# One outgoing transfer instead of four, four returning transfers instead of one: the block exchange through DRAM in an attention and expert kernel

## The chip, the cores and the metric

The kernel runs on one core of a Trainium2 chip. The metric is the device time of one execution in microseconds (us), over several executions of the same program. The core has five instruction queues that run beside each other and meet only at semaphores: TensorE (PE, matrix products), VectorE (DVE), ScalarE (ACT), GpSimd (POOL) and SyncE (SP). SP does no arithmetic here; it starts transfers. ACT computes, and it can start transfers too.

## The reference

32 sequences of 112 tokens of width 256 attend to their own context of 375 rows. The context rows and the latents together make 487 keys, with 16 heads of width 64. A mixture of eight experts follows, of which each token uses two. All of it is float32.

```python
x_ = layer_norm(x, ln_m_g, ln_m_b); lat = layer_norm(latents, ln_l_g, ln_l_b)
q  = lat @ Wq;  k, v = split(concat([x_, lat], 1) @ Wkv, 2)
dots = einsum('bhid,bhjd->bhij', q, k) * scale
attn = softmax(dots, axis=-1)
out  = einsum('bhij,bhjd->bhid', attn, v) ... @ Wout
x = x + tanh(g_xattn[0]) * out
# then: gate, top 2 of 8 experts, gelu MLP of width 1024, weighted sum, residual
x = x + tanh(g_ffn[0]) * ffn(layernorm(x))
```

The change touches only how the softmax weights `attn` are turned, so that the keys lie on the partitions for the product with `v`.

## The kernel before

**Stages.** The attention part runs as 64 stages (`period` in the code), each made of two of the 128 half steps `n`. A stage works for two "sets" `s` (one per sequence of a pair), each with two pairs of heads, `p` = 0 and 1. Work is pipelined over the stages. In one stage the kernel

1. multiplies the weights of the stage's own two sets with the values (`attend`, line 600, 64 products), and ACT copies the result out (line 617);
2. computes the scores of the next stage's two sets (`scores`, line 536), takes the negated row maxima on DVE (line 546), and takes the exponentials on ACT (`exps`, line 555, eight instructions per stage);
3. lets PE compute key, value and query projections for later stages (lines 373, 434, 439). Their results are gathered by ACT copies (line 475), DVE additions (line 484) and POOL additions (line 487);
4. normalises the exponentials on ACT (`norm`, line 569, two instructions for each set and `p`; the four are named n00, n01, n10, n11 after set and `p`) and turns them in 32x32 blocks on DVE (`turn_blocks`, line 574: t00, t01, t10, t11);
5. sends the turned blocks to DRAM (`send_blocks`, line 580; s0 and s1 for the two sets) and takes them back, in the next stage, with the blocks on other partitions (`take_blocks`, line 587).

**What the exchange does.** After `turn_blocks` each 32x32 block is transposed in itself, but still lies at its old place. A set is a tile `ex` of 128 partitions and 2048 floats (8 KB on each partition, 1 MB together). Block (a, k), where a is the group of 32 partitions and k a group of columns, has to go to partition group k, column group a. That move is done by a write to a DRAM tile `turned` and a read back into `exT`. Before the change the write did the sorting: four transfers, one for each a, of 2 KB runs, into `turned[k, j, a, n]`. The read back was one plain transfer of 128 runs of 8 KB.

**Order.** The order on every engine is written out by hand. The table `PLAN` has ten entries, five for each half step, and gives the place of each piece between the others. Its first lines are

```python
PLAN = ("k1 q0 q1", "k6 v1 n00", "v6 v5 n01 t00", "k7 v7 n10 t01 k2 s0", "v2 k5 n11 t10", "v3 t11 s1", ...)
```

The two takes of a stage stand right behind the second entry, in the main loop:

```python
if h == 1 and not late and n < LAST - 2:
    for s in (n, n + 1):
        take_blocks(s)
```

So on an engine that takes part in `take_blocks`, its instructions come after those of "k6 v1 n00" and ahead of those of "v6 v5 n01 t00". On ACT the first piece behind that point is the copy of v5 (line 475), which POOL's addition (line 487) waits for; then come n01, n10, the copy of k5, and n11. Before the change all sends and takes are on SP, in the same order as the loads of the inputs (`load`, lines 274 and 278), of the expert weights that are prepared beside the attention (`piece_in`, lines 1375 and 1379), their results going out (`piece_out`, lines 1415 and 1419), and the residual rows (lines 626 and 651).

**Buffers.** There are three `ex` tiles, two `exT` tiles and four `turned` tiles. A take has to wait until `attend` has read the old `exT` and until the send of its own set has landed. `attend` of a stage waits for both takes that belong to it.

Of the kernel before, what the change touches and what calls it, by code (L numbers as in the profile page):

```python
# [23 lines left out]
def kernel(  # L24
# [20 lines left out]
    nc = tc.nc  # L45
# [38 lines left out]
    KTB, EXB, ETB = 4, 3, 2  # L84
# [18 lines left out]
    QB, QW, Q = 4, 32, S // 4  # L103
# [17 lines left out]
    turned = [dram.tile([QB, QW, QB, 2 * NCK * 2 * QW], F32, name=f"turned_{n}") for n in range(4)]  # L121
# [70 lines left out]
    if True:  # L192
# [309 lines left out]
        pss, nmx, sm, exT = {}, {}, {}, {}  # L502
# [3 lines left out]
        exs = [const.tile([P, QB, 2, NCK, 2, QW], F32, name=f"ex_{n}") for n in range(EXB)]  # L506
# [68 lines left out]

        def send_blocks(n, eng=nc.sync):


            for a in range(QB):
                eng.dma_start(  # L580
                    turned[n % 4][:, :, a, :].rearrange("k j n -> j k n"),
                    exs[n % EXB][a * QW : (a + 1) * QW].rearrange("j k q c h r -> j k (q c h r)"),
                )

        def take_blocks(n):
            exT[n] = soft.tile([P, QB, 2, NCK, 2, QW], F32, tag="exT", name=f"exT_{n}", bufs=ETB)
            nc.sync.dma_start(
                exT[n].rearrange("p a q c h r -> p (a q c h r)"),
                turned[n % 4].rearrange("k j a n -> (k j) (a n)"),
            )  # L590

        def attend(j):

# [930 lines left out]
        norm(1, 0)  # L1524
        turn_blocks(0, 1)
        send_blocks(0)
        units[0, 1][6]()
        norm(1, 1)
        turn_blocks(1, 0)
        weight_sums(0, 2)  # L1530
        units[0, 1][1]()
        turn_blocks(1, 1)
        send_blocks(1)
        units[1, 0] = seven(1, 0, 0)
        for kv, k in PROLOGUE:
# [17 lines left out]
        for n in range(LAST):  # L1553
# [17 lines left out]
            def step(what, period=period, beside=beside, qn=qn):  # L1571
                s, p = int(what[1]), int(what[-1])
                if what[0] == "q":
                    for j in qn:
                        q_unit(j // NG, j % NG + NG * s)
                elif what[0] in "kv":
                    at = beside[what[0]]
                    if at[1] < (UNITS, UNITS // 2)[at[0]]:
                        if at not in units:
                            units[at] = seven(*at)  # L1580
                        units[at][p - 1]()
                elif period + 1 < UNITS:
                    s += 2 * (period + 1)
                    if what[0] == "n":
                        norm(s, p)
                    elif what[0] == "t":
                        turn_blocks(s, p)
                    else:
                        send_blocks(s)
# [24 lines left out]
            k = n - 44  # L1614
# [89 lines left out]
            for h in range(5):  # L1704
                for what in PLAN[5 * late + h].split():
                    step(what)
                do(pe[h])
# [3 lines that stand above are left out]
                if h == 1:  # L1711
                    do(after)
                if h == 1 and n == LAST - 2:
                    for s in (n, n + 1):
                        take_blocks(s)
                if h == 4:
                    break
                then_ = soon_[:]
                del soon_[:]
                do(then_)  # L1720
                for part in dve[h]:
                    part()

                if outgoing and (h % 2 == 0 or n > LAST - NG):
                    outgoing.pop(0)()
                if extra and not (late and h > 1 and isinstance(extra[0], tuple)):
                    do(extra.pop(0))
# [3 lines left out]
        r, _ = route_parts(g, nc.vector)  # L1731
# [130 lines left out]
```

## Time and profile before

| | |
|---|---|
| median of three runs | 1907.17 us (1904.93 to 1913.34) |
| the profiled execution | 1907.72 us, span 1905.9 us |
| granted TensorE clock | 0.997 |
| PE busy | 1876.3 us, 98% of the span |
| DVE busy | 1353.5 us, 71% |
| ACT busy | 1136.4 us, 60% |
| POOL busy | 992.5 us, 52% |
| sends (line 580) | 512 transfers of 256 KB, all from SP |
| takes (line 587) | 128 transfers of 1024 KB, all from SP |
| DMA queue q1 (SP's) | 247232 packets, 413.31 MB, 73.6% of 16 engines' span |
| DMA queue q10 (ACT's) | 2288 packets, 2.12 MB, 0.4% |

Times on the page are microseconds. In a list of waits, a line names who waited, for whom, the total, how often, and the longest wait. In a timeline a line has the start, the length, the engine, the source line, the operation, output and input, and the number of instructions merged into it; in brackets stands the idle time of the engine just before and what ended it. "SPq" and "ACTq" rows are the issuing of transfers on the queues of SP and ACT; their length is the time for which that queue was occupied with issuing, and not the time until the data landed. In the tile view, three numbers with slashes are the shortest, median and longest duration in ns. In the view by windows, each line is one stretch with the busy time of PE, PEld, DVE, ACT and POOL, the granted clock, the share for which the DMA engines were busy, and the rate in GB/s.

The attention stages lie between about 60 and 1490 us and are some 20.5 to 27 us long each. The expert part follows.

### The profile page before, as it was taken

What the parts mean: (1) busy time and instruction counts of PE and PEld (TensorE: products, weight loads), DVE (VectorE), ACT (ScalarE), POOL (GpSimd) and SP (SyncE); (2) the same over time, 40 slices, a digit from 0 to 9 for tenths busy, and PEclk for the clock granted to TensorE, in tenths of its full rate; (3) what the DMA queues carried; (4) which work ended last, traced back from release to release, by engine and by line L of the source; (5) the groups of instructions that cost most, each with busy time, mean ns of one, the idle gap of its engine ahead of it and who ended that gap; (6) DMA issues with size and microseconds to landing.
All of it is one profiled execution on the core that took longest, in us unless ns stands there. A gap on an engine that the chain in (4) does not pass through costs nothing. (4 is left out here: it accounts for less than half of the span.)

```text
span 1905.9 us, 38258 instructions
## 1 busy us (share of the span) xinstructions
PE 1876.3 (98%) x12560; PEld 1433.5 (75%) x12560; DVE 1353.5 (71%) x2868; ACT 1136.4 (60%) x2718; POOL 992.5 (52%) x1475
## 2 busy tenths in 40 slices
PE   8999999999999999999999999999999999999998
PEld 4667777677777676777676777677677999999887
DVE  6787878787877878787878787878776477844111
ACT  5767666666776666667766666666756334434333
POOL 6433333435445746585556655753334588877212
PEclk9999999999999999999999999999999999999999
DMA  7777766767788888798979898896668786897872
GB/s 202 193 229 209 214 196 198 205 182 205 226 227 265 253 246 251 230 280 250 271 224 284 233 268 242 252 265 195 198 184 256 244 240 180 245 336 232 231 205 46
DMA packets 261049, 433.23 MB, mean 227 GB/s; under 512 B 30728, under 2 KB 149072, under 8 KB 244464
## 3 DMA queue, kind: packets, MB, share of 16 engines
q1 hardware_dynamic: 247232, 413.31, 73.6%
q0 software_dynamic: 11328, 15.33, 4.2%
q10 hardware_dynamic: 2288, 2.12, 0.4%
q8 instruction: 101, 1.65, 0.3%
q14 instruction: 100, 0.82, 0.1%
HBM read 301.37 MB, written 172.28 MB: 249 GB/s over the span
## 5 line engine op out<-in xcount | busy, mean ns | idle before, releaser
L555 ACT ACTIVATE ex<-bank,nmx 128x512 f32<-128x512 f32 x512 | 343.6, 697 | 85.7 <-DVE nmx L546 85.2
L569 ACT ACTIVATE ex<-ex,rc 128x512 f32<-128x512 f32 x512 | 342.7, 721 | 76.1 <-DVE rc L566 75.4
L546 DVE TENSOR_REDUCE nmx<-bank 128x1 f32<-128x487 f32 x512 | 298.6, 655 | 85.9 <-PE bank L536 83.6
L574 DVE STREAM_TRANSPOSE ex<-ex 128x1024 f32<-128x1024 f32 x256 | 314.9, 1230 | 19.5 <-ACT ex L569 15.7
L487 POOL TENSOR_TENSOR vv<-tmpv,vv 128x512 f32<-128x512 f32 x64 | 82.1, 1282 | 404.1 <-ACT vv L475 403.4
L536 PE MATMUL bank<-kT,qTs 64*128 64x487 f32 x1024 | 236.3, 588 | 3.0 <-DVE kvT L365 1.7
L600 PEld LDWEIGHTS bank<-exT,vv 128*64 128x64 f32 (+1 forms) x4096 | 198.9, 137 | 30.9 <-issue 22.6
L600 PE MATMUL bank<-exT,vv 128*64 128x112 f32 (+1 forms) x4096 | 213.0, 261 | 2.3 <-DMA exT<-turned 1.6
L617 ACT COPY outT<-bank 128x256 f32<-128x256 f32 (+3 forms) x160 | 40.0, 314 | 263.9 <-PE bank L600 258.8
L434 PE MATMUL bank<-tT,wkv_s 128*128 128x487 f32 x378 | 186.3, 575 | 0.5 <-ACT ex L555 0.5
L439 PE MATMUL bank<-wkv_s,tT 128*128 128x256 f32 x768 | 186.7, 379 | 0.0
L439 PEld LDWEIGHTS bank<-wkv_s,tT 128*128 128x128 f32 x768 | 144.8, 190 | 43.3 <-issue 21.4
L1164 POOL DMA_INDIRECT out_dram<-y,xs x60 | 93.5, 1558 | 154.0 <-DVE y L1191 77.9
L536 PEld LDWEIGHTS bank<-kT,qTs 64*128 64x128 f32 x1024 | 98.8, 187 | 99.2 <-issue 69.9
L1405 POOL TENSOR_TENSOR piece<-piece 128x128 f32<-128x128 f32 x256 | 116.9, 457 | 89.7 <-DMA piece<-in_L_ffn_w_dram 78.3
L439 PE MATMUL bank<-wkv,kvT 128*128 128x256 f32 x512 | 132.0, 380 | 0.8 <-ACT ex L555 0.6
L439 PEld LDWEIGHTS bank<-wkv,kvT 128*128 128x128 f32 x512 | 94.6, 190 | 50.5 <-issue 33.9
L484 DVE TENSOR_TENSOR kT<-bank,kT 128x487 f32<-128x487 f32 x189 | 120.8, 640 | 14.0 <-POOL kT L487 7.5
L434 PE MATMUL bank<-kvT,wkv 128*128 128x487 f32 x252 | 130.1, 598 | 0.0
L484 DVE TENSOR_TENSOR vv<-bank,vv 128x512 f32<-128x512 f32 x192 | 128.2, 668 | 1.8 <-POOL vv L487 0.2
L1219 ACT ACTIVATE h<-h,b 128x256 f32<-128x256 f32 x160 | 66.1, 495 | 91.9 <-DVE h L1230 53.2
L373 PEld LDWEIGHTS bank<-kvT,wq_sb 128*128 128x128 f32 x512 | 96.2, 188 | 28.9 <-issue 17.0
(296 smaller groups left out, 3718.2 us busy)
## 6 DMA issues: line engine op xcount, KB each, us to landing
turned<-ex SPq DMA_DIRECT2D x512, 256.0 KB
exT<-turned SPq DMA_DIRECT2D x128, 1024.0 KB
w<-in_L_ffn_w_dram SPq DMA_DIRECT2D x132, 256.0 KB
w_s<-ws SPq DMA_DIRECT2D x80, 256.0 KB
w_t<-ws SPq DMA_DIRECT2D x80, 256.0 KB
w_b2x<-in_L_ffn_w_dram SPq DMA_DIRECT2D x38, 512.0 KB
ws<-piece SPq DMA_DIRECT2D x64, 256.0 KB
cin<-in_ctx_dram SPq DMA_DIRECT2D x32, 336.0 KB
```

Of the source, the lines that this page charges most:

```text
L373: nc.tensor.matmul(ps, lhsT=wq_sb[:, k, i * P : (i + 1) * P], rhs=kvT[g][:, k, :, SC:NK], start=(k == 0), stop=(k == KD - 1),)
L434: nc.tensor.matmul(ps, lhsT=w[:, 0, i * P : (i + 1) * P], rhs=x[:, :NK], start=True, stop=True)
L439: nc.tensor.matmul(ps[:, c, :], lhsT=x[:, (2 * h + c) * P : (2 * h + c + 1) * P], rhs=w[:, 1, i * P : (i + 2) * P], start=True, stop=True,)
L484: nc.vector.tensor_tensor(v[o], ps, v[r], ALU.add)
L536: nc.tensor.matmul(ps[:, :NK], lhsT=qT[b // 2, i][r, b % 2].rearrange("p a i -> p (a i)"), rhs=kT[b, i][r, :], start=True, stop=True,)
L546: nc.vector.tensor_reduce(nmx[b, i][:, j : j + 1], pss[b, i][j][:, :NK], AX.X, ALU.max, negate=True)
L555: nc.scalar.activation(exs[n % EXB][:, :, p, :, j, :], ps[j].rearrange("p (c k r) -> p k c r", c=NCK, r=QW), AF.Exp, bias=nmx[b, i][:, j : ...
L569: nc.scalar.mul(t, t, rc[:, j : j + 1])
L574: nc.vector.transpose(t, t)
L600: nc.tensor.matmul(ps[y * DH : (y + 1) * DH, r, x * S : (x + 1) * S].rearrange("p (a i) -> p a i", a=QB), lhsT=vv[j // 2, c // 2][:m, c % ...
L1164: add = nc.gpsimd.indirect_dma_start(out=outf, out_offset=bass.IndirectOffsetOnAxis(ap=xs[t][:, b, D + 1 : D + 2].bitcast(I32), axis=0), i ...
L1405: nc.gpsimd.tensor_tensor(o, l, r, op) for o, l, r, op in ops
```

## The change

The sorting moves from the write to the read. The tile `turned` is now read as `[a, j, k, n]`: a send writes the whole `ex` tile as it lies, in one transfer of 128 runs of 8 KB. A take is four transfers, one for each destination group of 32 partitions, and each of the four gathers 128 runs of 2 KB. The first two are issued by SP and the last two by ACT. The same bytes move in each direction, and nothing else of the kernel is edited.

```diff
         def send_blocks(n, eng=nc.sync):

-
-            for a in range(QB):
-                eng.dma_start(
-                    turned[n % 4][:, :, a, :].rearrange("k j n -> j k n"),
-                    exs[n % EXB][a * QW : (a + 1) * QW].rearrange("j k q c h r -> j k (q c h r)"),
-                )
+            eng.dma_start(
+                turned[n % 4].rearrange("a j k n -> (a j) (k n)"),
+                exs[n % EXB].rearrange("p k q c h r -> p (k q c h r)"),
+            )

         def take_blocks(n):
             exT[n] = soft.tile([P, QB, 2, NCK, 2, QW], F32, tag="exT", name=f"exT_{n}", bufs=ETB)
-            nc.sync.dma_start(
-                exT[n].rearrange("p a q c h r -> p (a q c h r)"),
-                turned[n % 4].rearrange("k j a n -> (k j) (a n)"),
-            )
+            for k in range(QB):
+                eng = (nc.sync, nc.scalar)[k // 2]
+                eng.dma_start(
+                    exT[n][k * QW : (k + 1) * QW].rearrange("p a q c h r -> p a (q c h r)"),
+                    turned[n % 4][:, :, k, :].rearrange("a j n -> j a n"),
+                )
```

Per stage SP issues six of these transfers instead of ten, and ACT four instead of none.

## The prediction

> **What bounds the kernel now.** I read the page first (who is busy, who moves the bytes), then the list of waits, then one stage as a timeline, then DMA by windows.
>
> ```profile
> PE 1876.3 (98%) x12560; PEld 1433.5 (75%) x12560; DVE 1353.5 (71%) x2868; ACT 1136.4 (60%) x2718; POOL 992.5 (52%) x1475
> ```
>
> TensorE has work in 98% of the span, so a shorter transfer can win only what PE waits for transfers. Anything that makes another engine late is paid in full once its cover is used up.
>
> ```profile
> POOL vv L487 <- ACT vv L475: 403.4, 60, 13.5
> ACT ex L569 <- DVE rc L566: 75.4, 87, 2.4
> DVE nmx L546 <- PE bank L536: 83.6, 45, 3.2
> PEld bank L434 <- ACT ex L555: 45.5, 64, 1.3
> ```
>
> The first line: once in nearly every stage POOL stands still until ACT has copied v5, the copy that stands right behind the new ACT transfers. The third is the cover: in 45 of some 62 stages DVE is idle for 1.86 us (83.6/45) before its first row maximum; in the other 17 it comes there late already. The fourth: in all 64 stages the first weight load behind the scores waits for an exponential, which waits for a maximum. A late DVE is therefore felt by PE in the same stage.
>
> ```profile
> L580 SPq DMA_DIRECT2D turned<-ex x512: 302/691/1981, 34.0 to 1468.8; - x171
> L587 SPq DMA_DIRECT2D exT<-turned x128: 319/412/1715, 41.3 to 1479.8; - x128
> ...
>   DMA exT<-turned: 3.4, 2
> ```
>
> The tile view of the exchange: a send of 128 runs of 2 KB occupies SP for 0.69 us, a take for 0.41. The last line is how long the products waited for takes: twice, 3.4 us together. The exchange is hidden.
>
> ```profile
> 273.57 1.33 ACT L569 ACTIVATE ex<-ex,rc 128x512 f32<-128x512 f32 x2
> 274.81 0.58 ACT L475 COPY vv<-bank 128x512 f32<-128x512 f32 x1
> 275.30 1.33 ACT L569 ACTIVATE ex<-ex,rc 128x512 f32<-128x512 f32 x2
> 277.32 1.22 DVE L574 STREAM_TRANSPOSE ex<-ex 128x1024 f32<-128x1024 f32 x1
> 284.34 0.13 DVE L523 MEMSET bank<- 128x25 f32 x3
> 286.59 3.52 DVE L546 TENSOR_REDUCE nmx<-bank 128x1 f32<-128x487 f32 x6 [2.12 <-PE bank L536]
> 282.24 3.30 PE L600 MATMUL bank<-exT,vv 128*64 128x112 f32 x64
> ```
>
> One stage (261.6 to 282.2, from products to products). n00 runs at 273.57, the v5 copy at 274.81, n01 at 275.30. The new transfers stand between the first two lines. DVE has no gap from 274.94 to 284.4, then waits 2.12 us for scores.
>
> ```profile
> 274.00:275.00 1.00, 1.00 (x5) 0.73 (x4) 0.83 (x3) 1.00 (x3) 0.00 (x0) 1.00 0.97 410
> ...
> 280.00:281.00 1.00, 1.00 (x5) 0.67 (x4) 1.00 (x2) 1.00 (x2) 0.92 (x2) 1.00 0.99 197
> ```
>
> Last two columns: DMA share and GB/s. Takes (274) run at 410, sends (280) at 197, each with the DMA engines full. From 276 to 279 they are nearly idle.
>
> **The change part by part.** The sum is made against the profiled execution, 1907.7 us, which is 0.5 above the median of 1907.2.
>
> *Removed from SP:* 512 sends become 128, and 128 takes become 256. Per stage SP loses 8 x 0.69 + 2 x 0.41 = 6.3 us of issuing and gets back 2 sends at 0.4 (the row of the 8 KB takes) and 4 takes at 0.69 = 3.6. The 2.7 us are worth nothing on the path: SP stood waiting for turned blocks for 545.5 us (89 waits at line 580 for DVE), and nothing waits for SP but transfers, whose lateness cost PE 3.4 us at line 600 and 1.8 us of weight loads. Gain: 0 to 5 us; I take 0, since neither wait recurs by stage.
>
> *The sends' runs grow from 2 to 8 KB.* No row writes 8 KB runs to DRAM. Bounds: 197 GB/s as now, or 410 as the 8 KB reads have it: 1.05 MB in 5.3 or 2.6 us. The take of the next stage is the earliest reader, some 5 us behind the last send, so both are hidden: 0.
>
> *Added to ACT:* four issues per stage, 256 in all. They stand behind n00 and, in one stage of four, behind the two activations of line 361, and ahead of the v5 copy, n01, n10, the k5 copy and n11. Price of four issues together:
>
> ```profile
> 2.29 0.36 ACTq L1435 DMA_DIRECT2D wkv<-in_L_xattn_Wkv_dram  x1
> 2.69 0.44 ACTq L1435 DMA_DIRECT2D wkv_s<-in_L_xattn_Wkv_dram  x1
> 3.17 1.72 ACTq L1435 DMA_DIRECT2D wkv<-in_L_xattn_Wkv_dram  x2
> ...
> 1515.13 2.24 SPq L1092 DMA_DIRECT2D w_t<-ws  x4
> ...
> 741.18 4.54 SPq L580 DMA_DIRECT2D turned<-ex  x4
> ```
>
> Four on ACT's own queue take 0.36 + 0.44 + 1.72 = 2.52 us; four reads of 2 KB runs on SP 2.24; four sends behind a busy queue 4.54, the upper end. The lower end is four single ones at 0.343 (the shortest issue on ACT, at line 936): 1.4. I take 2.5, the row of this queue. Part runs beside ACT's arithmetic: at 1672.11 a transfer is issued 0.3 us before the activations of 1671.51 end, so the queue runs ahead by 0.3 to at most one activation (0.67); I take 0.5. So v5 and all behind it on ACT is 2.0 us later, with 0.7 and 4.5 as ends. The takes' own waits add nothing here: the send landed long before, and `attend`, which frees exT, ended some 9 us earlier.
>
> *Who waits for ACT.* First DVE: the transpose t01 (277.32) needs n01 (ends 276.63), cover 0.7. In other stages that cover is 0.1 (t01 at 256.17, n01 ends about 256.1) or 1.2 (207.37 against 206.13). With 0.7 as the mean, DVE's tail is 1.3 us later. In the 45 stages with 1.86 us of idle time that is absorbed; in the 17 without it reaches the maxima, the exponentials and PE: 17 x 1.3 = 22 us. Ends: 0 at a delay of 0.7; at 4.5 us, 3.8 x 17 + (3.8 - 1.86) x 45 = 152 us.
>
> Second POOL: from 713.42 (v5's addition) to 723.50 it has no gap, and DVE waits 0.21 us for it at 721.02. In such stages (pieces, tokens and input sums on POOL, about every third, 20) the whole 2.0 arrive, against covers of 1.4 to 2.0, and 0 in three of them: 0.4 on average, 8 us. Ends: 0, and 20 x (4.5 - 1.4) = 62, which overlaps the 152.
>
> *PE's own waits.* The first product of each set waits for four transfers instead of one, six more wait instructions per stage. One is 51 ns at line 600 where the trace has it: 62 x 6 x 0.051 = 19 us if none runs ahead, 0 if all do (the weight loads' short waits, 0.44 us each at line 600, cost the products next to nothing). I take 6. The exponentials lose as many waits (17 to 38 ns each) on ACT, which is worth nothing on PE's path.
>
> *Transfers that come later.* The ACT takes start some 10 us later in the stage than SP's do. By the stage above they are issued from 274.4 to 277 and needed at 282.24 (first set) and 283.1 (second). At 410 GB/s 1.05 MB take 2.6 us, at 197 GB/s, the rate of 2 KB runs in the sends, 5.3. With 2.6 us from the last issue to the landing (sends end issuing at 265.69, the take that needs them is issued at 268.33) they land by about 279.6, or 281 to 282.3. Hidden by the first, just hidden by the second. I take the first, since reads of 2 KB runs (w_s and w_t, 1518 to 1520) move 382 GB/s. Cost 0; the other end is a rival below.
>
> Sum: 22 + 8 + 6 = 36 us: 1907.7 + 36 = 1943.7, or 1943 against the median.
>
> *A rule against the change.* The Trainium skill (DMA: Bandwidth & Descriptors, Rules for kernel authors) advises against splitting a transfer into disjoint partition groups: the parts run on the same engines and one transfer for all partitions is better. The rows above have the engines full with one take (0.97), which agrees, but they hold no split take. By the rule the split brings 0 in transfer time and only adds issues, so the sum stays; by the trace alone it could also have cost 2.7 us per set, the difference of the two rates. A second statement there (Anatomy of one DMA) is a time of 2.0 us and 1 us for each 436 KB, for the other kind of queue: by an estimate from it the last 256 KB would land 2.6 us after issue, and the late rival would not happen at all.
>
> **The rivals.**
>
> *Hidden after all (not slower).* If ACT's queue takes the issues while n00 still runs and each costs the single price, the delay is 0.7 us and ends in t01's cover of 0.7. For it: 0.343 single issues, and idle DMA from 276 to 279. Against it: no row of four stays under 1.5 us. It decides at a delay of 0.7. Time: 1907 to 1913; 1910.
>
> *Late takes.* If gathered 2 KB reads run at 197 GB/s and share the engines with weight pieces or s0, the products wait 1 to 3 us in each stage, in place of, not beside, most of the tail's delay: 62 x 1 to 62 x 3, 1970 to 2094. Against it: the 382 GB/s row, and that s0 is itself later by ACT's delay.
>
> *Faster.* Shorter sends end the 5.2 us of waits for exT: 1902, if ACT's cost is hidden too. To be told from no change it must win 9.5 us, so another 4 us would have to come from POOL's 78.3 us of waiting for weight pieces, which PE has felt little so far: 1898.
>
> **How the numbers follow.** About 0.5%, 9.5 us, can be told from no change. Chances: forecast mechanism (1918 to 1985) 0.52; hidden 0.22; late takes or an ACT delay near its upper end 0.19; faster 0.07. The hidden case is all within 0.5%. The range must reach into the hidden case and part of the late one: 1906 to 2010 leaves out the faster case and a little over half of the last one. Faster 0.07, same 0.22, slower 0.71.
>
> **What would show it.** ACTq rows of line 587 with about 2.5 us per four; the gap between n00 and v5 grown by about 2 us; POOL's wait for ACT at L487 up by 60 x 2 = 120 us; the line "DVE nmx <- PE" clearly below 83.6; PE's wait for exT still a few us; 8 KB sends visible as a changed rate where 197 stands now. Wrong it would be if the ACT gap is under 1 us, or if products wait for exT in every stage.

## The result, and the profile after

The changed kernel takes 1932.26 us (median; 1929.57 to 1934.45), the kernel before on the same chip 1907.76 us (1904.93 to 1913.34). The ratio is 1.0124, with a 95% interval of 1.0096 to 1.0153: slower by some 24.5 us. The profiled execution took 1934.26 us, its span is 1932.6 us, 26.7 more than the span before.

Page of the changed kernel, engines and the two DMA queues (packets, MB, share of 16 engines' span):

```profile
PE 1886.4 (98%) x12560; PEld 1437.9 (74%) x12560; DVE 1357.2 (70%) x2868; ACT 1139.2 (59%) x2718; POOL 991.5 (51%) x1475
...
q1 hardware_dynamic: 210368, 346.18, 60.6%
q10 hardware_dynamic: 39152, 69.24, 16.9%
```

The same bytes of these two queues now keep the DMA engines busy for 77.5% of the span instead of 74.0%. One of the two directions has become dearer.

List of waits of the changed kernel:

```profile
POOL vv L487 <- ACT vv L475: 442.1, 57, 15.3
DVE nmx L546 <- PE bank L536: 85.6, 44, 5.0
PE bank L600 <- DMA exT<-turned: 11.6, 15, 2.0
```

POOL waits 39 us more for ACT's v5 copy (403.4 before), not 120. DVE's wait for scores has not shrunk (83.6 before): DVE comes to its maxima as early as it did. The products at line 600 now wait for takes.

Tile `exT` of the changed kernel (shortest, median, longest in ns, first and last start; then idle time of its engines before the instructions on that tile, and how often):

```profile
L587 ACTq DMA_DIRECT2D exT<-turned x256: 309/442/1734, 50.4 to 1502.0; - x128
...
  DMA exT<-turned: 17.3, 21
```

3.4 us in two waits has become 17.3 us in 21, products and weight loads together; PE's own part is 1.6 us before and 11.6 now. The median issue on ACT takes 0.44 us.

Timeline of ACT in the stage that the prediction showed (now 265.2 to 285.8):

```profile
277.12 0.31 ACTq L587 DMA_DIRECT2D exT<-turned  x1
277.13 0.72 ACT L569 ACTIVATE ex<-ex,rc 128x512 f32<-128x512 f32 x1
277.47 0.45 ACTq L587 DMA_DIRECT2D exT<-turned  x1
...
278.04 0.85 ACTq L587 DMA_DIRECT2D exT<-turned  x2
278.93 0.59 ACT L475 COPY vv<-bank 128x512 f32<-128x512 f32 x1 [0.47 <-issue]
```

The four issues occupy the queue from 277.12 to 278.89. They begin together with n00, not behind it, and run beside it for 1.3 us. From the start of n00 to the v5 copy it is 1.80 us, against 1.24 before (273.57 to 274.81): the copy is 0.56 us later. Over the 33 stages in which this copy follows n00 directly, the median of the same time is 1.99 us, 0.75 more than before, and the longest 3.60.

Windows of the same stretch:

```profile
268.00:269.00 1.00, 1.00 (x15) 0.64 (x12) 0.00 (x0) 0.47 (x3) 1.00 (x2) 1.00 0.96 385
...
274.00:275.00 1.00, 1.00 (x8) 0.96 (x7) 0.26 (x2) 1.00 (x5) 0.00 (x0) 1.00 1.06 201
...
281.00:282.00 1.00, 1.00 (x6) 0.70 (x5) 1.00 (x1) 0.95 (x2) 0.97 (x1) 1.00 1.06 217
```

Sends (268) now move at 385 GB/s, takes from SP (274) at 201 and from ACT (281) at 217, with the DMA engines full in all three. Before, the takes ran at 410 and the sends at 197. The slow rate has changed sides: it lay on the sends, which nobody waits for soon, and lies on the takes, which the products wait for.

**Where the 26.7 us lie.** I took the first product of each of the 64 stages from the timelines and compared the stages one by one (before the change they are 19.8 to 30.7 us long). Stages without weight pieces have the length that they had, to 0.01 us in most (20.17, 21.07, 28.03, 21.26, 20.62 us in both kernels); of stages 1 to 25, five are longer, by 1.9 us together. The loss by part of the span, for this kernel and for those of the experiments below whose parts were compared:

| us more than the kernel before | stages 0-25 | 26-51 (pieces) | 52-61 | 62 | behind the start of 63 | span |
|---|---|---|---|---|---|---|
| the change | 4.6 | 15.1 | -1.2 | 4.3 | 3.9 | 26.7 |
| all takes on SP (e1) | 2.0 | 3.7 | -0.7 | 3.2 | 6.2 | 14.5 |
| ACT in piece stages only (e9) | 0.2 | 17.8 | -0.6 | 2.7 | 5.2 | 25.4 |
| ACT outside of them only (e10) | 1.7 | 7.6 | -1.4 | 5.3 | 7.7 | 20.9 |
| all on SP, last pair as before (e11) | -0.2 | 6.4 | -0.6 | 1.5 | 6.1 | 13.2 |
| pieces and last pair as before (e12) | 3.1 | 0.3 | 1.3 | 1.4 | 0.2 | 6.3 |

The table sets single executions beside one of the kernel before that was among its faster ones: 1907.72 us, where the median of that kernel beside e9 to e12 is 1911.43. By the medians e12, for one, is 1.6 us slower and not 6.3.

One stage with pieces shows how. Weight loads of TensorE in the kernel before, from the first product of stage 46, through its first score, to the first product of stage 47:

```profile
1102.76 3.09 PEld L600 LDWEIGHTS bank<-exT,vv 128*64 128x64 f32 x64 [0.72 <-issue]
1106.50 0.19 PEld L536 LDWEIGHTS bank<-kT,qTs 64*128 64x128 f32 x2 [0.21 <-issue]
...
1123.83 0.29 PEld L600 LDWEIGHTS bank<-exT,vv 128*64 128x64 f32 x6 [0.72 <-issue]
```

The same in the changed kernel:

```profile
1116.60 0.80 PEld L600 LDWEIGHTS bank<-exT,vv 128*64 128x64 f32 x16 [1.34 <-issue]
1119.56 3.77 PEld L600 LDWEIGHTS bank<-exT,vv 128*64 128x64 f32 x48 [2.16 <-issue]
1123.99 0.19 PEld L536 LDWEIGHTS bank<-kT,qTs 64*128 64x128 f32 x2 [0.21 <-issue]
...
1141.31 0.77 PEld L600 LDWEIGHTS bank<-exT,vv 128*64 128x64 f32 x16 [0.72 <-issue]
```

From the scores to the next products it is 17.33 us before and 17.32 after, although ACT issues four transfers in between. All that is lost is lost among the products: 64 loads in one run become 16, a gap of 2.16 us, and 48 slower ones. The second set's blocks had not landed. They are on their way from 1104.69 on: SP issues its half, then two pieces, and ACT its half at 1107.22 to 1110.55. Issues of SP in this stage, then windows:

```profile
1104.69 1.96 SPq L587 DMA_DIRECT2D exT<-turned  x4
1106.81 2.54 SPq L1375 DMA_DIRECT2D piece<-in_L_ffn_w_dram  x2
...
1108.00:1110.00 2.00, 2.00 (x9) 1.43 (x8) 1.85 (x4) 0.63 (x2) 0.00 (x0) 1.00 1.06 186
...
1114.00:1116.00 2.00, 2.00 (x7) 0.95 (x5) 2.00 (x5) 1.08 (x3) 1.92 (x3) 1.00 1.07 197
```

Engines full without a gap, at 186 to 206 GB/s in all four windows of these 8 us. Both halves are 2.1 MB, or 10.5 us at 200; the pieces add 0.26 MB and 1.3 us; from 1104.7 that ends at 1116.5, and the products were due at 1116. In fact the second set's products started at 1119.59: from 1115.35 on the next send and a piece going out move beside the rest. In the kernel before, a window of this stage has 402 GB/s, at which the same 2.1 MB take 5.2 us:

```profile
1094.00:1098.00 4.00, 4.00 (x16) 2.84 (x16) 3.31 (x7) 3.14 (x6) 2.85 (x5) 1.00 1.00 402
```

The 48 products are also slow because TensorE's granted clock fell to half just there:

```profile
1119.59 3.96 PE L600 MATMUL bank<-exT,vv 128*64 128x112 f32 x48 [1.98 <-DMA exT<-turned]
...
1119.20:1122.60 3.40, 3.01 (x33) 3.04 (x35) 0.41 (x4) 0.00 (x0) 3.10 (x6) 0.50 1.04 407
```

At full clock 48 such products take 2.53 us (stage 63, at 1512.46), so some 1.4 of the 3.65 us that the products of this stage lost are the clock's.

Over stages 26 to 51, what the products of line 600 lost inside their run sums to 10.3 us, what they lost in front of the first one (a gap above 0.72 us, as the 1.34 above) to 3.2. Together that is 13.5 of the 15.1 us, in the products of eight stages (26, 27, 30, 34, 38, 42, 46 and 50). The rest, 1.6 us in stages 43 and 51, is all that ACT's delay can have cost there.

In these eight stages SP issued its first take 11.6 to 14.7 us ahead of the products, and 14.8 us or more ahead in every other stage from 2 to 62 but number 54. There it was 12.1 us, but the only piece is one going out ahead of the takes, and none comes in behind them; the stage is 0.05 us longer. So both the short lead and the pieces seem to be needed.

**The clock elsewhere.** Stretches at half clock, of 3.4 us or a multiple, stand at a few places in every trace, the one before too. In the first stage ten score products wait for DVE; the change, and then e12, which has the same code there:

```profile
66.54 3.97 PE L536 MATMUL bank<-kT,qTs 64*128 64x487 f32 x10 [1.88 <-DVE kvT L365]
...
67.70 2.71 PE L536 MATMUL bank<-kT,qTs 64*128 64x487 f32 x10 [1.92 <-DVE kvT L365]
...
67.90:74.70 6.80, 6.80 (x15) 3.73 (x12) 3.32 (x6) 5.60 (x18) 0.00 (x0) 0.50 0.55 117
...
67.90:74.70 6.80, 6.80 (x29) 4.17 (x28) 4.81 (x9) 6.31 (x20) 0.00 (x0) 1.00 0.66 149
```

The first stage is 27.3 to 27.6 us long in the change and in e1, e6 and e7, with 6.8 us at half clock in it; 25.7 before and in e5, with 3.4; and 24.0 to 24.3 in e8 to e12, with none. So nearly all of the 1.9 us that the change loses in this stage is the clock's. Why one execution falls to half clock behind an idle time of 1.9 us and another does not is open.

Stage 62 lost its 4.3 us to half clock (1494.6 to 1501.5, up to 3.4 us) and to a wait for gathered expert rows, which was 1.25 us before:

```profile
1496.58 1.12 PE L1115 MATMUL bank<-ident,xs 128*128 128x128 f32 x4 [4.42 <-DMA xs<-xg]
```

For the takes of the last pair the products of the change waited 1.34 us, 1.59 before. Why the rows came later was not settled.

### The profile page after: what moved, and what is told of

It reads as the page before. It is cut to its first block, busy times and chain, and to the rows that moved or that the text cites. A ratio compares the mean times of both kernels' runs of the same rounds, so it can differ in the third digit from the quotient of the medians.

```text
span 1932.6 us, 38353 instructions
## 1 busy us (share of the span) xinstructions
PE 1886.4 (98%) x12560; PEld 1437.9 (74%) x12560; DVE 1357.2 (70%) x2868; ACT 1139.2 (59%) x2718; POOL 991.5 (51%) x1475
## 5 line engine op out<-in xcount | busy, mean ns | idle before, releaser
L546 DVE TENSOR_REDUCE nmx<-bank 128x1 f32<-128x487 f32 x512 | 298.4, 655 | 85.9 <-PE bank L536 85.6
L600 PE MATMUL bank<-exT,vv 128*64 128x112 f32 (+1 forms) x4096 | 214.9, 262 | 12.1 <-DMA exT<-turned 11.6
L1405 POOL TENSOR_TENSOR piece<-piece 128x128 f32<-128x128 f32 x256 | 116.9, 457 | 46.4 <-DMA piece<-in_L_ffn_w_dram 34.8
```

The lines of the kernel that those rows point to most:

```text
L546: nc.vector.tensor_reduce(nmx[b, i][:, j : j + 1], pss[b, i][j][:, :NK], AX.X, ALU.max, negate=True)
L600: nc.tensor.matmul(ps[y * DH : (y + 1) * DH, r, x * S : (x + 1) * S].rearrange("p (a i) -> p a i", a=QB), lhsT=vv[j // 2, c // 2][:m, c % ...
L1405: nc.gpsimd.tensor_tensor(o, l, r, op) for o, l, r, op in ops
```

## The experiments

**e1: all takes on SP.** Layout and transfers of the change, without ACT.

```diff
-                eng = (nc.sync, nc.scalar)[k // 2]
+                eng = nc.sync
```

> All four takes of a set are issued by SyncE, otherwise the changed kernel. Theory A (late takes: ScalarE's half is issued some 10 us into the stage, moves at about 200 GB/s because its 2 KB runs are gathered, and lands after the products are due where weight pieces share the engines): the takes start as early as in the kernel before, the waits of the products for exT fall from 17.3 us to under 6 us, and the time returns to 1905 to 1913 us. Theory B (ScalarE's issuing delays its copies, VectorE and GpSimd, and so TensorE): the time returns too, 1905 to 1913. Theory C (2 KB gathered reads cost DMA time whoever issues them): it stays at 1925 or above.

Measured: 1922.78 us (1921.51 to 1923.61), ratio 1.0064 (1.0047 to 1.0080). Half of the loss stays without a single issue on ACT. The windows at 273 to 277 have 201 to 238 GB/s at a DMA share of 1.02 to 1.09: the rate belongs to the layout, whoever issues. By the table, the stages with pieces lose 3.7 us, all inside the products, and the last pair 3.2. There PE's first 16 products come behind a gap of 4.44 us (0.72 before), and its timeline goes on with the other 48, at half clock (1493.6 to 1503.9):

```profile
1500.46 4.16 PE L600 MATMUL bank<-exT,vv 128*64 128x112 f32 x48 [3.07 <-DMA exT<-turned]
```

Here the products of the last pair stand in front of their data (3.07 us, 1.59 before). So the theory that ACT's queue is the whole cost falls.

**e2: the old layout, its take split.** Sends and layout of the kernel before; each take becomes four transfers of 32 partitions with runs of 8 KB, two of them on ACT.

```diff
-            nc.sync.dma_start(
-                exT[n].rearrange("p a q c h r -> p (a q c h r)"),
-                turned[n % 4].rearrange("k j a n -> (k j) (a n)"),
-            )
+            for k in range(QB):
+                eng = (nc.sync, nc.scalar)[k // 2]
+                eng.dma_start(
+                    exT[n][k * QW : (k + 1) * QW].rearrange("p a q c h r -> p a (q c h r)"),
+                    turned[n % 4][k],
+                )
```

> The kernel before with its sends and layout, but each take split into four transfers of 32 partitions, two of them from ScalarE at the place of the changed kernel. Its reads are contiguous runs again. Theory A: the late half moves at about 400 GB/s, lands 2 to 3 us earlier, the waits for exT stay under 6 us, 1906 to 1915 us, while ScalarE's queue still issues four transfers per stage. Theory B: the issuing is the same, so it is as slow as the changed kernel, 1925 to 1940. If 32 partitions and not the runs make the reads slow, the DMA windows show about 200 GB/s in the takes and it is slow by theory A too.

Measured: 2087.13 us (2080.31 to 2093.08), ratio 1.0934 (1.0913 to 1.0954). No theory had that. Two things come out of it. First, a window in which only ACT's queue moves bytes, its takes of 8 KB runs (224 GB/s over 283 to 286), with the engines full:

```profile
285.00:286.00 1.00, 1.00 (x5) 0.68 (x4) 1.00 (x4) 0.66 (x2) 0.80 (x2) 1.00 0.98 197
```

8 KB runs in groups of 32 partitions move at 197, and the same runs in one transfer of 128 partitions at 410 in the kernel before. So it is not the length of the runs. Second, the waits of the two queues:

```profile
SPq L589 <- DMA exT<-turned: 308.9, 41, 13.9
...
SPq L580 <- DMA exT<-turned: 107.9, 64, 11.2
```

SP stands 417 us before issues until earlier takes have landed, and ACT's v5 copy up to 7.3 us for the same reason. The granted clock of this execution is 0.969, against 0.997 before, so a part of its loss is the clock's. In the program as built, the transfers share eight semaphores in rotation, so that one can wait for the landing of the one eight before it, whichever queue that went by. With 16 slow transfers per stage on two queues the two hold each other up. That this rotation is the reason of the waits is inferred from the rows; what supports it is e5, which also has 16 per stage, on one queue, and loses nothing.

**e3: ACT's half earlier.** The two transfers per set go ahead of the stage's loop, right behind the exponentials; SP's half stays.

```diff
+            if not late and n < LAST - 2:
+                for s in (n, n + 1):
+                    take_blocks(s, range(2, 4))
             for h in range(5):
...
-                        take_blocks(s)
+                        take_blocks(s, range(2))
```

> The changed kernel with ScalarE's two transfers of each set issued about 3 us earlier in its order, right behind the eight exponentials, ahead of the copies of k1 and v1 and of n00; SyncE's half stays. Theory A: about 3 us of lateness go, the longest waits for exT (2 to 3.6 us per stage) vanish, 1912 to 1922 us. Theory B: four issues still stand ahead of v5's copy and now also ahead of k1's and v1's, so 1930 or more.

Measured: 1996.52 us (1995.25 to 1999.26), ratio 1.0454 (1.0436 to 1.0471). The products wait for takes only twice now (4.1 us), but ACT stops. Its timeline, where three of the four transfers are out by 591.49:

```profile
597.91 0.31 ACTq L588 DMA_DIRECT2D exT<-turned  x1
598.26 0.57 ACT L475 COPY kT<-bank 128x487 f32<-128x487 f32 x1 [6.83 <-DMA exT<-turned]
```

The fourth transfer could not be issued before earlier data have landed, and it stands in ACT's instruction stream. All of ACT's arithmetic behind it waits 6.8 us. In the windows 592 to 598 both halves are issued, and 172 to 196 GB/s move with the engines full. By queue it is one after the other: from 592 to 594 SP's moves 0.38 MB and ACT's 0.01, from 595 to 598 SP's 0.02 and ACT's 0.55. A second queue with other partition groups added nothing to the slow rate here.

**e4 and e6: ACT later, without transfers.** All takes on SP as in e1, and in the place of ACT's issues some copies of 128 x 128 that nobody reads: eight of them (2.59 us in ACT's timeline, the v5 copy 2.49 us later), or two (0.63 us, 0.54 later).

```diff
-                eng = (nc.sync, nc.scalar)[k // 2]
+                eng = nc.sync
...
                     for s in (n, n + 1):
                         take_blocks(s)
+                    for _ in range(8):
+                        nc.scalar.copy(busy, ones)
```

> All four takes from SyncE, as in the first of these, and in the place of ScalarE's four issues eight small copies of a constant into a spare tile, about 2 us of ScalarE time per stage: the delay that the prediction assumed, without any late transfer. Theory B as predicted: 36 us over the first of these, about 1943. Theory A: a delay of 2 us is nearly absorbed by VectorE's idle time in most stages; 1908 to 1925.

> All takes from SyncE and two small copies (about 0.5 us) instead of eight in the place of ScalarE's issues: the size of the gap that the changed kernel really shows ahead of v5's copy. Theory: a delay of this size is absorbed, 0 to 6 us over the kernel with all takes on SyncE, 1921 to 1929. If the delay costs in proportion, 73 x 0.5/2.1 = 17 us, 1940.

Measured: with eight 1995.65 us (1994.14 to 1999.56), ratio 1.0446 (1.0429 to 1.0464); with two 1928.01 us (1924.16 to 1931.86), ratio 1.0096 (1.0073 to 1.0119). Against e1 that is 73 us and 5 us. So a delay of 2.49 us cost 1.15 us in each of some 63 stages, and one of 0.54 us next to nothing in most stages: plain stages keep their lengths but for numbers 13 and 14 (0.7 and 1.4 us, part of it at half clock, 377.8 to 381.2). The cover behind ACT is real and lies between the two. The change's own delay, 0.56 us in the stage shown and 0.75 in the median, is near the lower of the two.

**e5: split by columns.** The kernel before, each take in four transfers that reach all 128 partitions, with runs of 2 KB, all from SP.

```diff
+            for a in range(QB):
+                nc.sync.dma_start(
+                    exT[n][:, a].rearrange("p q c h r -> p (q c h r)"),
+                    turned[n % 4][:, :, a, :].rearrange("k j n -> (k j) n"),
+                )
```

> The kernel before with its sends, each take split into four transfers of all 128 partitions by columns instead of by partitions: 128 runs of 2 KB, 8 KB apart in DRAM, all from SyncE. It separates two readings of the 200 GB/s that the changed kernel's takes show. If short gathered runs are slow: about 200 GB/s in the DMA windows right behind the takes. If transfers that touch only 32 partitions are slow, which the earlier run with 8 KB runs into 32 partitions at about 200 GB/s speaks for: 380 to 420 GB/s. Its time is not the point; 1908 to 1930.

Measured: 1910.54 us in one run, with 1909.46 for the kernel before on that chip. Its windows while takes move:

```profile
273.00:274.00 1.00, 1.00 (x7) 0.87 (x6) 0.54 (x2) 1.00 (x4) 0.00 (x0) 1.00 1.01 309
...
276.00:277.00 1.00, 1.00 (x5) 0.70 (x5) 1.00 (x3) 0.81 (x2) 0.94 (x1) 1.00 0.98 377
```

Four transfers of 2 KB runs reach 291 to 377 GB/s if each touches all partitions, and some 200 if each touches 32. The shorter runs cost something (410 for one take of 8 KB runs), the partition groups cost the half. Splitting as such, with four waits for each product instead of one, costs nothing that the time shows.

**e7: more bytes beside the takes.** The change, and in the plain stages two transfers of 256 KB from DRAM to DRAM behind SP's takes.

```diff
+                    if 6 <= n <= 40:
+                        for c in range(2):
+                            nc.sync.dma_start(spare[c], w1[n % E, c * P : (c + 1) * P, :512])
```

> The changed kernel with two extra copies of 256 KB from DRAM to DRAM in each of the 18 stages from the fourth to the twenty-first, where there are no weight pieces, issued by SyncE right behind its takes. Theory A (ScalarE's half is late where other traffic fills the engines ahead of it): stages that were as long as in the kernel before get 0.3 to 3.5 us longer each, and products wait there for exT: 1940 to 1985. If traffic is not what makes it late, those stages keep their lengths, 1930 to 1935.

Measured: 1932.29 us in one run, as the change without them; the plain stages keep their lengths. It did not make the takes late, so the test that was to show the part of other traffic did not show it; the windows say why:

```profile
296.00:298.00 2.00, 2.00 (x10) 1.60 (x9) 1.84 (x6) 2.00 (x5) 0.00 (x0) 1.00 0.09 22
298.00:303.00 5.00, 5.00 (x21) 3.22 (x20) 4.82 (x9) 3.70 (x8) 2.57 (x2) 1.00 0.94 204
```

The extra bytes were gone before ACT issued at 296.90 (share 0.09 from 296 to 298); its half moved alone from 298 to 303 and was there in time. The dose was too small and too early. How many bytes it takes in a plain stage was not measured; in stage 45, with pieces, 0.26 MB stand between SP's half and ACT's half, directly in front of the latter, with SP's half itself only 2.5 us ahead. That the traffic makes the difference rests on such rows and on stage 54, not on a run that added it.

**e8: the last pair from SP.** The change, with the takes of the last two sets all on SP.

```diff
-                eng = (nc.sync, nc.scalar)[k // 2]
+                eng = nc.sync if n >= LAST - 2 else (nc.sync, nc.scalar)[k // 2]
```

> The changed kernel with only the last two sets taken wholly by SyncE, whose ScalarE issues stood for 13.9 us ahead of the first experts' copy. Theory: the stall of that copy goes, 2 to 5 us less than the changed kernel, 1927 to 1931; the rest of its loss, in the stages with pieces, stays.

Measured: 1937.15 us (1935.26 to 1937.90), ratio 1.0149 (1.0132 to 1.0166): not faster. In the changed kernel ACT's timeline has, at the last pair,

```profile
1488.43 13.88 ACTq L587 DMA_DIRECT2D exT<-turned  x4
...
1504.00 0.58 ACT L1222 COPY h<-bank 128x512 f32<-128x512 f32 x1 [15.29 <-PE bank L1212]
```

With SP issuing, that copy runs at 1496.24. The 13.9 us for which ACT's queue was blocked looked costly, but without them the kernel is no faster. Eight issues on SP last from 1495.87 to 1501.72 instead and push the first expert weights back.

**e9 and e10: ACT's half in some stages only.** Sets 52 to 107 belong to the stages with pieces. In e9 ACT issues for these alone, in e10 for all others but the last two.

```diff
-                eng = (nc.sync, nc.scalar)[k // 2]
+                eng = (nc.sync, nc.scalar)[k // 2] if 52 <= n < 108 else nc.sync
```

> ACT issues its half only for sets 52 to 107, whose products lie in the stages with the expert weights' pieces; SP issues everything elsewhere. Reading 1 (the loss of the changed kernel beyond the all-SP kernel is ACT's half landing late where the DMA engines are full): the piece stages lose their 15.5 us again, the start about 2 and the end 9 as with all takes on SP, together 1931 to 1936. Reading 2 (it is spread over all stages as small delays of ACT): about half of the 10 us between the two kernels returns, 1926 to 1929, and the piece stages lose under 10 us.

> The complement: ACT issues its half for all sets but 52 to 107 and the last two. Reading 1: the piece stages lose only the 4 us of the all-SP kernel, and the others nothing by ACT, 1921 to 1925. Reading 2: 1926 to 1930.

Measured: e9 1934.52 us (1933.11 to 1939.14), ratio 1.0132 (1.0112 to 1.0152); e10 1932.08 us (1924.38 to 1934.61), ratio 1.0107 (1.0088 to 1.0126). By place the first reading holds: ACT in the stages with pieces loses 17.8 us there, in the table's row of e9, and in e10 ACT in the plain stages loses 1.8 in stages 1 to 25, where e1 loses nothing. By the totals it does not: e10 lies above both expectations. Its profiled execution, 1928.54, loses 7.6 us in the stages with pieces and 13.0 at the end, where its code is that of e1, which lost 3.7 and 9.4. e11 has the same code in the stages with pieces too, and lost 6.4. What SP's own slow takes cost there is thus 4 to 8 us, from one execution to another, and ACT's part in the change some 7 to 11 of the 15.1. Some 1.7 us of e10's 7.6 are the clock's: in stage 34 it is at half from 839.9 to 843.3, and 48 products take 4.18 us there.

**e11 and e12: the old exchange where it hurts.** In e11 all takes are on SP and the last two sets are exchanged as in the kernel before. In e12 sets 52 to 107 and the last two are, and all others as in the change, with ACT's half. `old` stands for these sets.

```diff
+            if old:
+                for a in range(QB):
+                    eng.dma_start(
+                        turned[n % 4][:, :, a, :].rearrange("k j n -> j k n"),
+                        exs[n % EXB][a * QW : (a + 1) * QW].rearrange("j k q c h r -> j k (q c h r)"),
+                    )
+                return
...
+            if old:
+                nc.sync.dma_start(
+                    exT[n].rearrange("p a q c h r -> p (a q c h r)"),
+                    turned[n % 4].rearrange("k j a n -> (k j) (a n)"),
+                )
+                return
```

> All takes on SP, and the last two sets are exchanged as in the kernel before (four sends of 2 KB runs, one take of 8 KB runs). If the 8.8 us that the all-SP kernel loses in the last pair and the expert part come from the slow takes of the last pair, they go: 1912 to 1915. If they come from elsewhere (weights that a different order of transfers brings later): no change, 1921 to 1924.

> Sets 52 to 107 and the last two are exchanged as before; all others as in the change, with ACT's half. If the change costs nothing where the engines have room and nobody is at the end, what is left is the 2 to 3 us of the first stages: 1908 to 1913. If four issues on ACT cost something per stage in the plain stages after all, 36 of them at 0.3 us or more: 1920 or more.

Measured: e11 1920.12 us (1915.08 to 1921.79), ratio 1.0041 (1.0025 to 1.0058); e12 1913.07 us (1911.12 to 1917.12), ratio 1.0015 (1.0005 to 1.0025), in runs beside 1911.43 for the kernel before. e12 says where the loss is not: 35 stages in which ACT issues four transfers each cost 0.15% together. e11 missed its first expectation. Stage 62 is mended (1.5 instead of 3.2), but the part behind it is 6.1 us longer, as in e1, though its exchange there is the old one. In e12 that part has its old length. Two `w_t` loads come later in e11 (PE waits 2.5 us for them, 0.2 before), as do the last products; why they are late with the takes of earlier sets on SP was not settled.

## Why the prediction was right, and where it was not

The sign and the size came out: 1932 against 1943, inside the range. The path to the number was mostly wrong: a term put at zero carries about half of the loss, and the terms that made the sum are nearly gone. That the sum came so near is luck.

- *SP relieved, worth 0.* Nothing gained shows but 1.3 us in stage 61, which were not followed up. Right.
- *Sends of 8 KB, worth 0.* They run at 385 GB/s, near the upper bound given, and nobody felt it. Right.
- *Four issues on ACT, 2.5 us, less 0.5.* Measured 1.77 us in the stage shown, less 1.3 that run beside n00. The delay is 0.56 us there and 0.75 in the median, not 2.0. The row of four issues at the kernel's start was too dear and the overlap too small; the lower end given was 1.4 less at most 0.67.
- *DVE's tail, 22 us, and POOL's chain, 8 us.* Within the stages with pieces at most 1.6 us, and 1.9 us over the plain stages 1 to 25 (number 13 alone 0.54), of which 0.8 are late takes of stage 2. The sign asked for, DVE's wait clearly below 83.6, did not come (85.6), and POOL's wait grew by 39 us, not 120. The covers were mis-sized as well: in e4 a delay of 2.49 us cost 73 us, where the prediction's covers give 30 for DVE's tail (17 x 1.79) and, by an estimate from its 1.4 to 2.0, some 20 for POOL. Two errors, one in the delay and one in the covers, worked against each other.
- *PE's extra waits, 6 us.* Plain stages equal to 0.01 us, and e5: 0.
- *Late takes, 0.* This step failed: 13.5 us in eight stages, 1.4 of them by the clock in one. The prediction chose 382 GB/s for the gathered takes, from a row of 2 KB reads (`w_s`, `w_t`), over 197 from the old sends. It asked which row was alike in direction and run length. The row alike in what counts was the send: one transfer for each 32 partitions. e2 (8 KB runs, 32 partitions, 197) and e5 (2 KB runs, 128 partitions, 291 to 377) show that. The lead was misread too: ACT's half does not start some 10 us behind SP's but 6 by the prediction's own rows (268.33 and 274.4), 7.2 in the change. With the lower rate the prediction's own working gave "just hidden" for a plain stage, and that is what happened there; the stages with pieces, where other transfers stand between the halves, were named in the rival and not worked out.
- *Not in the sum.* No term had the clock, nor the end: the first stage lost 1.9 us, stage 62 and what lies behind it 8.2.

The rivals: *hidden* set its condition at a delay of 0.7 us, and ACT about met it (0.56 and 0.75); its time was missed because of the takes. *Late takes* had the mechanism, with the condition as it was found (2 KB gathers at 197, shared with pieces), but put it in every stage and so at 1970 at least. It was true of eight stages with pieces, 13.5 us, and not of the last pair, where the wait for takes is no longer than before. *Faster* failed, although POOL's wait for weight pieces fell (78.3 to 34.8 us): PE did not feel it. Its 5.2 us of waits also counted the 1.8 us of weight loads twice: the 3.4 us are 1.6 of PE and 1.8 of weight loads.

The rule of the Trainium skill (DMA: Bandwidth & Descriptors, Rules for kernel authors) against two transfers to disjoint partition halves was weighed as a split that "only adds issues". It was right, and as weighed too mild: the groups of 32 halve the rate (201 against 410 GB/s). By the prediction's estimate from that page's other statement (Anatomy of one DMA), the late rival would not happen at all; here ACT's last issue ended at 278.89 and the engines stayed full at 184 to 264 GB/s until 283, so the measurement decides against using it for these transfers.

Open are the 4 to 8 us behind the last pair, in the change and in e1, e9, e10 and e11, but not in e12. By the stretches at half clock there, the clock explains at most 2.9 us of it (in e9, 9.2 us at half clock against 3.4 before), and nothing in the change.

## What to carry to other kernels

When a transpose goes through DRAM, the direction that is read under a deadline gets the whole transfer over all partitions, and the sorting goes to the side that nobody waits for. To price a transfer for which there is no row, take the row that shares its number of partitions first, and its run length after that. An average margin says little: work out the bytes between issue and need in the stage with the most other traffic, since here stages 1 to 25 lost 1.9 us together and eight full ones 13.5.

## What the runs showed of the hardware that was not expected

- The rate goes by the partitions that a transfer touches: 32 of them 197 to 217 GB/s in the windows shown, with runs of 2 or 8 KB (180 to 264 in single windows of 1 us), 128 of them 291 to 377 with 2 KB and 385 to 410 with 8 KB, the DMA engines full each time.
- A second queue with transfers to other partition groups added nothing: 172 to 196 GB/s in all with both halves issued, and the halves moved one after the other (e3).
- Four issues on ACT cost its arithmetic 0.56 us, not their 1.77, since the queue starts on them with the activation in front. But a transfer that may not be issued yet stops the arithmetic behind it: 6.8 us in e3, up to 2.3 us in the change.
- Taking a queue's stop of 13.9 us away won nothing where the transfers then stood in the other queue (e8), and a gap of 2.16 us in the products cost 3.65 us in all, since half clock came behind it.
- TensorE's granted clock falls to 0.50 for 3.4 to 10.2 us a few times in a trace. In the first stage that makes 24.0 to 24.3, 25.7 or 27.3 to 27.6 us of the same work, with 0, 3.4 or 6.8 us at half clock.
